# Attention's softmax transposed in float32 for two head pairs at a time, and cross attention queries over 512 weight columns

## The chip, the cores and the metric

The kernel runs on one core of a Trainium2 chip. The metric is the device time of one execution in microseconds (us), taken as the median of several runs. A profiled execution is traced beside them: every instruction on TensorE (PE; its weight loads are shown as PEld), VectorE (DVE), ScalarE (ACT), GpSimd (POOL) and on SyncE's DMA queue (SP), with its start, its duration and what ended the idle time before it. Line numbers such as L878 are those of the kernel before the change; the kernel after is a few lines shifted from `q_stream` on.

## The reference, cut to what matters

A two-layer decoder on 16 sequences of 64 tokens, width 512. Layer 0 has a causal attention with 32 query heads on 8 kv heads of width 128, a linear attention over channels with the context, and a gated ffn with group-scaled int4 weights. Layer 1 has an attention with ALiBi bias, a cross attention to the context and a base product with gated low-rank experts. A LayerNorm follows every block (post-LN). The part that the change touches is the attention of both layers and the queries of layer 1's cross attention:

```python
# attention, for every batch, kv head h and its four query heads g
s = einsum('bhgnd,bhmd->bhgnm', q, k) / sqrt(128) + mask    # 64 x 64
p = softmax(s, axis=-1)
o = einsum('bhgnm,bhmd->bhgnd', p, v)
x = layernorm(x + o @ wo.T)
# cross attention: the queries are normalised before the scores
q = rmsnorm(x @ q_proj_w.T)      # per head of 128
```

## The kernel before, in words

**Numbers.** Most products must be as good as float32, but TensorE works on fp32r, a rounded 32-bit type. A float32 matrix is therefore split into hi (rounded to fp32r, a cast on ACT) and lo (the exact rest, a subtraction on POOL or DVE). A product is then three matmuls, hi x hi + hi x lo + lo x hi (`mm3`, L101 to L107). `split_sb` (L84) splits from SBUF with ACT and POOL, `split_ps` (L89) from PSUM with ACT and DVE.

**Tiles.** The 1024 tokens are eight tiles of 128 (two batches each), in two halves of 512. SBUF tiles come from pools by tag, with a number of buffers each (`BUFS`, L34): `st` takes every loaded weight block before its split, `wq` and `wo` hold split weights, `s` and `p` softmax tiles, `pts` the transposed softmax, `ot` the attention's output split in hi and lo. PSUM has eight banks: two `mm`, three `fx`, one each of `sc` (scores), `pt` (transposes), `o` (product with V).

**Attention.** `Stream.run` (L970) walks a list of (layer, half of the tokens, kv head), two steps for each entry and four batches for a step: 32 steps for L0 and 64 for L1 (self attention, then cross attention), 96 in all. A step s does, in program order:
- projections of a later head (`units`), `fill` (work of other parts of the network that is spread over the steps),
- `pt(s, 0)`: four transposes of the softmax of two batches and a copy to `pts`; then the output projection `oproj(s - 1, 0)` of the step before (12 matmuls of 512 columns); then `av(s, 0)`, the product with V,
- more `fill` and projections, and the same for the other two batches: `pt(s, 1)`, `oproj(s - 1, 1)`, `av(s, 1)`,
- `scores(s + 2)`: 8 small matmuls and the softmax of the step after the next.

**Softmax.** `scores` (L847) leaves a tile `x` of [128 rows (two query heads, 64 queries), 8 (batch, pair of heads), 64 keys] in float32. The row maximum, the subtraction, exp, the sum and the division take DVE, ACT and POOL. Before the change, `x` is then split on ACT and POOL into `p`, hi and lo side by side on 128 columns (L871, L872). `pt` (L874) transposes each 128 x 128 block of `p` in fp32r, so that the hi of the 64 keys lands on partitions 0 to 63 and the lo on 64 to 127. V lies on both halves of the partitions, so one matmul over 128 partitions adds hi and lo.

**Cross attention queries.** `qn_front` (L790) computes the queries of one token tile for four heads in one bank, in two groups of 256 columns, one for each pair of heads: 24 matmuls of 256 columns. The weight `wqx` comes in two blocks a head, by pairs of query heads (L1056). ACT squares, DVE sums, POOL takes the power -1/2 and DVE multiplies (`rms`, L154); `qn_back` (L803) transposes.

**Linear attention.** `q_stream` (L359) runs chunks of 128 channels through five stages that lie 0, 1, 2, 4 and 5 ticks behind the first: logits, exp, norm, transpose, out (L430). Its tiles alternate between the tags `s` and `p` (L378). Beside the L0 ffn, a tile `acc` of tag `p` (L503) holds partial sums.

**Order.** Tile, the framework, puts the instructions of every engine into an order at build time, by priority and by when its own cost model expects operands to be ready. Softmax and the evacuations around it get a higher priority (`soon`, L74). Each engine then runs its list in that order. So the order on an engine is fixed before the run, and may differ from the program's.

## Time and profile before

Three runs took 2276.78, 2277.01 and 2281.83 us, median 2277.01. The profiled execution has a span of 2275.4 us from its first to its last instruction; the granted TensorE clock was 0.994 of full speed on average.

| stretch of the profiled execution (us) | what runs | PE busy | DVE | ACT | POOL |
|---|---|---|---|---|---|
| 0 to 45 | first loads and projections | 39.0 | 15.8 | 23.3 | 22.0 |
| 45 to 430 | L0 attention, keys of the linear attention | 382.5 | 221.1 | 231.5 | 159.4 |
| 430 to 740 | L0 attention, queries of the linear attention | 305.7 | 191.4 | 152.3 | 168.9 |
| 740 to 1150 | L0 ffn, rest of the queries, context keys and values | 381.6 | 337.1 | 214.4 | 230.2 |
| 1150 to 1660 | L1 self attention | 507.8 | 197.5 | 229.0 | 252.2 |
| 1660 to 2240 | L1 cross attention and L1 ffn | 564.2 | 357.8 | 267.6 | 336.0 |
| 2240 to 2276 | last LayerNorms and outputs | 27.8 | 25.4 | 6.0 | 4.2 |

Groups that matter below, with the number of instructions, the busy time in us and the mean duration of one in ns:

| line | engine, what | count | busy | mean |
|---|---|---|---|---|
| L878 | PE, fp32r transposes of p | 768 | 91.6 | 241 |
| L807 | PE, float32 transposes of queries | 256 | 38.5 | 273 |
| L105 | PE, hi x hi of the cross attention's queries, 256 columns | 512 | 149.3 | 292 |
| L889 | PE, product with V | 768 | 125.0 | 285 |
| L86 | ACT, hi of p | 96 | 59.6 | 620 |
| L87 | POOL, lo of p | 96 | 124.3 | 1295 |
| L881 | ACT, copy of the transposed softmax | 192 | 113.0 | 588 |
| L92 | DVE, lo of ot from PSUM | 192 | 132.0 | 687 |

How to read it: "busy" is the union of the durations in a group, and matmuls are pipelined, so the duration of one is longer than the distance to the next. Idle time is given before the instruction that ended it, with the releaser. On an engine that isn't the bottleneck idle time costs nothing.

### The profile page before, as it was taken

The page shows a single profiled execution, that of the slowest core. Times are in us where ns is not written, and L with a number is a line of the kernel's source. Part 1 is how long each engine was busy: PE and PEld are TensorE (multiplying, and loading weights), DVE is VectorE, ACT ScalarE, POOL GpSimd, SP SyncE. Part 2 cuts the span into 40 slices and gives each one's busy share as a digit, 9 for nine tenths or more (in the row PEclk, how much of TensorE's full clock was granted, in tenths as well). Part 3 has the DMA queues.
Part 4 walks back from the last instruction along what each step waited for, and adds up shares of the span by engine and source line. Part 5 has one row for each costly group of instructions (what it writes and reads, how often), then busy time and mean ns, then how long its engine had stood idle before and what let it go on. Part 6 is the DMA issues. An engine that isn't in the chain of part 4 may idle for free.

```text
span 2275.4 us, 36680 instructions
## 1 busy us (share of the span) xinstructions
PE 2208.5 (97%) x13200; PEld 1917.7 (84%) x13200; DVE 1346.0 (59%) x2523; ACT 1124.1 (49%) x2195; POOL 1172.9 (52%) x1001
## 2 busy tenths in 40 slices
PE   8999999999999999999999999999999999999998
PEld 7888888888888777777788888888898899988996
DVE  3655555667645789887743343433356566666656
ACT  5665556555444455555444444444444454443442
POOL 3533334455554655464654554545455666554641
PEclk9999999999999999999999999999999999999999
DMA  7533333322334322456543443334333343332320
GB/s 231 158 115 109 112 105 120 110 84 77 91 114 154 120 83 86 153 180 184 156 144 106 131 126 119 116 111 140 107 113 101 115 123 99 103 105 85 112 70 29
DMA packets 255317, 267.24 MB, mean 117 GB/s; under 512 B 32672, under 2 KB 168352, under 8 KB 255136
## 3 DMA queue, kind: packets, MB, share of 16 engines
q1 hardware_dynamic: 255136, 264.90, 38.1%
q8 instruction: 105, 1.72, 0.3%
q14 instruction: 76, 0.62, 0.1%
HBM read 231.26 MB, written 33.55 MB: 116 GB/s over the span
## 4 chain that ended last, share of the span: by engine, by line
PE 79%; DMA 5%; DVE 5%; POOL 5%; issue 2%; ACT 2%; SPq 0%; POOLq 0%; DVEq 0%; ACTq 0%
PE mm L105 16%; PE mm L106 15%; PE mm L107 15%; PE sc L856 6%; PE o L889 4%; PE fx L105 3%; PE fx L107 3%; PE fx L106 3%; PE pt L878 2%; DMA st<-in_down_s 1%; POOL wo L87 1%; PE fx L325 1%; POOL wq L87 1%; PE fx L298 1%; PE fx L316 1%
## 5 line engine op out<-in xcount | busy, mean ns | idle before, releaser
L87 POOL TENSOR_TENSOR wq<-st,wq 128x512 fp32r<-128x512 f32 x200 | 263.7, 1331 | 329.2 <-ACT wq L86 326.1
L107 PE MATMUL mm<-wo,ot 128*128 128x512 f32 x896 | 352.2, 393 | 0.0
L87 POOL TENSOR_TENSOR wo<-st,wo 128x512 fp32r<-128x512 f32 x226 | 296.6, 1342 | 96.8 <-ACT wo L86 88.0
L105 PE MATMUL mm<-wo,ot 128*128 128x512 f32 x768 | 315.2, 410 | 3.4 <-DVE x L904 3.1
L904 DVE TENSOR_TENSOR x<-x,mm 128x512 f32<-128x512 f32 x192 | 131.1, 683 | 308.2 <-PE mm L107 307.8
L106 PE MATMUL mm<-wo,ot 128*128 128x512 f32 x768 | 301.1, 392 | 0.0
L105 PE MATMUL mm<-xth,wq 128*128 128x512 f32 x512 | 204.9, 400 | 0.6 <-DVE v L92 0.3
L106 PE MATMUL mm<-xtl,wq 128*128 128x512 f32 x512 | 200.9, 392 | 0.0
L107 PE MATMUL mm<-xth,wq 128*128 128x512 f32 x512 | 200.6, 392 | 0.0
L107 PEld LDWEIGHTS mm<-wo,ot 128*128 128x128 f32 x896 | 169.3, 189 | 37.1
L91 ACT CAST ot<-o 128x512 fp32r<-128x512 f32 x192 | 112.3, 585 | 174.6 <-PE o L889 173.6
L114 POOL TENSOR_TENSOR r<-e,nhalf 128x4 f32<-128x4 f32 (+1 forms) x96 | 88.6, 923 | 203.2 <-DVE e L113 194.2
L86 ACT CAST wq<-st 128x512 fp32r<-128x512 f32 x204 | 123.8, 620 | 130.7 <-PE mm L106 73.5
L856 PEld LDWEIGHTS sc<-kt,qt 128*128 128x128 f32 x1536 | 184.4, 193 | 3.1
L856 PE MATMUL sc<-kt,qt 128*128 128x64 f32 x1536 | 185.0, 273 | 0.0
L92 DVE TENSOR_TENSOR ot<-o,ot 128x512 fp32r<-128x512 f32 x192 | 132.0, 687 | 81.8 <-ACT ot L91 81.5
L870 POOL TENSOR_TENSOR s<-s,rc 128x512 f32<-128x512 f32 x96 | 100.6, 1048 | 141.7 <-DVE rc L869 77.4
L105 PEld LDWEIGHTS mm<-wo,ot 128*128 128x128 f32 x768 | 144.6, 188 | 27.9 <-DVE x L904 3.4
L106 PEld LDWEIGHTS mm<-wo,ot 128*128 128x128 f32 x768 | 145.3, 189 | 24.1
L86 ACT CAST wo<-st 128x512 fp32r<-128x512 f32 x226 | 129.7, 624 | 41.0 <-PE mm L106 21.9
L105 PE MATMUL fx<-wq,xth 128*128 128x256 f32 x512 | 149.3, 292 | 0.0
L107 PE MATMUL fx<-wq,xtl 128*128 128x256 f32 x512 | 145.5, 284 | 0.0
(283 smaller groups left out, 5626.1 us busy)
## 6 DMA issues: line engine op xcount, KB each, us to landing
st<-in_wq SPq DMA_DIRECT2D x128, 256.0 KB, 3.1
st<-in_wo SPq DMA_DIRECT2D x128, 256.0 KB, 3.1
vs<-v SPq DMA_DIRECT2D x256, 128.0 KB, 3.1
v<-v SPq DMA_DIRECT2D x128, 128.0 KB, 2.7
st<-in_wqx SPq DMA_DIRECT2D x64, 256.0 KB, 2.9
st<-in_wox SPq DMA_DIRECT2D x64, 256.0 KB, 3.4
vs<-xv SPq DMA_DIRECT2D x128, 128.0 KB, 3.0
st<-in_gu_q SPq DMA_DIRECT2D x56, 256.0 KB, 3.0
```

What stands on the lines that cost most here:

```text
L86: self.nc.scalar.copy(hi, src)
L87: (self.nc.vector if fast else self.nc.gpsimd).tensor_tensor(lo, src, hi.bitcast(F32), ALU.subtract)
L91: self.nc.scalar.copy(hi, src)
L92: self.nc.vector.tensor_tensor(lo, src, hi.bitcast(F32), ALU.subtract)
L105: self.nc.tensor.matmul(out, lh, rh, start=first and i == 0, stop=False)
L106: self.nc.tensor.matmul(out, lh, rl, start=False, stop=False)
L107: self.nc.tensor.matmul(out, ll, rh, start=False, stop=last and i == n - 1)
L114: self.nc.gpsimd.tensor_tensor(out, e, self.nhalf[:, :n], ALU.pow)
L856: nc.tensor.matmul(sc[:, i * 64:(i + 1) * 64], qt[:, c + b, gp * 128:(gp + 1) * 128], kt[:, (c + b) * 64:(c + b + 1) * 64], start=True, st ...
L870: nc.gpsimd.tensor_tensor(x, x, rc.unsqueeze(2).to_broadcast([128, 8, 64]), ALU.mult)
L889: nc.tensor.matmul(o[:, b * 256:(b + 1) * 256], self.vs[s][i][:, bp * 2 + b], pts[:, b * 256:(b + 1) * 256], start=i == 0, stop=i == 1)
L904: self.nc.vector.tensor_tensor(n.x[t], n.x[t], ps, ALU.add)
```

## The change

The split of the softmax moves behind the transposition. `scores` leaves the normalised `x` in float32. `pt` is called once in a step: it transposes four blocks of 128 columns, each the two head pairs of one batch side by side, in float32. The transposed block then has the keys of one head pair on partitions 0 to 63 and those of the other on 64 to 127. For each pair, ACT copies its 64 partitions to fp32r as hi, and DVE writes the difference as lo to the other 64 partitions. So hi and lo again lie on the two halves, for the first pair in one order, for the second in the other. Both products with V of the step read from this tile.

The cross attention's query weights are arranged by halves of the input width instead of pairs of heads: a block has 2 of the 4 input parts and all 512 columns. `qn_front` is 12 matmuls of 512 columns.

Buffers: `st` 6 to 5, `s` 3 to 4, `ot` 4 to 3; a `pts` tile is twice as large. `q_stream` takes its softmax tiles from `p` alone, two chunks in one tile, and transposes three ticks behind the logits instead of four; `out` follows at four instead of five. The comments are gone from the file.

```diff
-BUFS = {"st": 6, "wq": 6, "wo": 6, "wk": 2, "wv": 2, "v": 4, "vs": 4, "qt": 2, "kt": 2, "s": 3, "p": 3, "pts": 2, "ot": 4}
+BUFS = {"st": 5, "wq": 6, "wo": 6, "wk": 2, "wv": 2, "v": 4, "vs": 4, "qt": 2, "kt": 2, "s": 4, "p": 3, "pts": 2, "ot": 3}
...
@@ q_stream, logits
-            s = live[c] = self.t(("s", "p")[c % 2], [128, 8, 64])
+            if c % 2 == 0:
+                cur["s"] = self.t("p", [128, 2, 8, 64])
+            s = live[c] = cur["s"][:, c % 2]
...
-        stages = ((5, out), (4, transpose), (2, norm), (1, exp), (0, logits))
+        stages = ((4, out), (3, transpose), (2, norm), (1, exp), (0, logits))
...
@@ qn_front
-        for gp in range(2):
-            w = self.wqs[h, gp]
-            n.mm3(ps[:, gp * 256:(gp + 1) * 256], [n.xt_slices(t, k) + (w[0][:, k], w[1][:, k]) for k in range(4)])
+
+        ws = [[flat(w).rearrange("p (k c) -> p k c", k=2) for w in self.wqs[h, kp]] for kp in range(2)]
+        n.mm3(ps, [n.xt_slices(t, k) + (ws[k // 2][0][:, k % 2], ws[k // 2][1][:, k % 2]) for k in range(4)])
...
@@ scores
-            x = n.t("s", [128, 8, 64])
+            x = self.p[s] = n.t("s", [128, 8, 64])
...
-            p = self.p[s] = n.t("p", [128, 8, 128], FR)
-            n.split_sb(x, p[:, :, 0:64], p[:, :, 64:128])
-
-    def pt(self, s, bp):
+
+    def pt(self, s):
+
         n, nc = self.n, self.nc
-        pt = n.bank("pt", FR)
-        for i in range(4):
-            nc.tensor.transpose(pt[:, i * 128:(i + 1) * 128], self.p[s][:, bp * 4 + i], n.identr)
-        pts = n.t("pts", [128, 512], FR)
+        pt, x = n.bank("pt"), self.p.pop(s)
+        for b in range(4):
+            nc.tensor.transpose(pt[:, b * 128:(b + 1) * 128], flat(x[:, 2 * b:2 * b + 2]), n.ident)
+        pts = n.t("pts", [128, 4, 256], FR)
         with n.soon():
-            nc.scalar.copy(pts, pt.bitcast(F32))
+            for gp in range(2):
+                r, q = slice(gp * 64, gp * 64 + 64), slice(64 - gp * 64, 128 - gp * 64)
+                src, c = pt[r].rearrange("p (b q) -> p b q", b=4), slice(gp * 128, gp * 128 + 128)
+                nc.scalar.copy(pts[r, :, c], src)
+                nc.vector.tensor_tensor(pts[q, :, c], src, pts[r, :, c].bitcast(F32), ALU.subtract)
         return pts
...
@@ av
-                                 pts[:, b * 256:(b + 1) * 256], start=i == 0, stop=i == 1)
+                                 pts[:, bp * 2 + b], start=i == 0, stop=i == 1)
...
@@ run
-            a = self.pt(s, 0)
+            a = self.pt(s)
...
-            a = self.pt(s, 1)
...
@@ _arrange
-    r["wqx"], r["wox"] = inout(i["L1_xattn_q_proj_w"].T, pairs), out(i["L1_xattn_o_proj_w"].T)
+    r["wox"] = out(i["L1_xattn_o_proj_w"].T)
...
+    r["wqx"] = inout(i["L1_xattn_q_proj_w"].T, KV).reshape(KV, 128, 2, 1024).transpose(0, 2, 1, 3)
```

More of the change, by code (lines that the diff above doesn't have):

```diff
@@ L1075, in _arrange @@
     r["b_base"], r["b_thr"] = i["L1_ffn_b_base"].reshape(1, D), i["L1_ffn_b_thr"].reshape(1, 1)
-    for n in ("wq0", "wq1", "wqx"):
+    for n in ("wq0", "wq1"):
         r[n] = r[n].reshape(KV, 2, 128, 1024)
+    r["wqx"] = inout(i["L1_xattn_q_proj_w"].T, KV).reshape(KV, 128, 2, 1024).transpose(0, 2, 1, 3)
     return {n: c(v) for n, v in r.items()}
```

## The prediction

> **What bounds the kernel now.** I read the engines' busy shares first, then the waits, then the timeline around the code that changes. The page's first part:

> ```profile
> span 2275.4 us, 36680 instructions
> PE 2208.5 (97%) x13200; PEld 1917.7 (84%) x13200; DVE 1346.0 (59%) x2523; ACT 1124.1 (49%) x2195; POOL 1172.9 (52%) x1001
> ```

> TensorE (PE) is busy 97% of the span, and the stage windows (0, 45, 430, 740, 1150, 1660, 2240 us) give it 382 of 385, 306 of 310, 382 of 410, 508 of 510 and 564 of 580 us. So a cut in PE's own work shortens the run directly, and a cut elsewhere only where PE waits. The idle 67 us lie mostly at the start, in the L0 ffn (740 to 1150 us, VectorE (DVE) 337 of 410 us busy) and in the cross attention (1660 to 2240). The page's durations of single matmuls overlap, so prices here are distances between starts. The timeline of PE shows both parts of the change in one look:

> ```profile
> 1703.26 0.28 PE L106 MATMUL fx<-wq,xth 128*128 128x256 f32 x1
> 1703.38 0.29 PE L107 MATMUL fx<-wq,xtl 128*128 128x256 f32 x1
> 1703.51 0.46 PE L878 MATMUL pt<-identr,p 128*128 128x128 f32 x4
> 1703.80 0.46 PE L105 MATMUL mm<-wo,ot 128*128 128x512 f32 x1
> 1704.10 0.39 PE L106 MATMUL mm<-wo,ot 128*128 128x512 f32 x1
> 1704.33 0.39 PE L107 MATMUL mm<-wo,ot 128*128 128x512 f32 x1
> ...
> 1713.08 0.64 PE L889 MATMUL o<-pts,vs 128*128 128x256 f32 x4
> 1713.55 0.60 PE L807 MATMUL fx<-ident,s 128*128 128x128 f32 x4
> 1713.91 0.36 PE L105 MATMUL fx<-wq,xth 128*128 128x256 f32 x1
> 1714.11 0.28 PE L106 MATMUL fx<-wq,xth 128*128 128x256 f32 x1
> ```

> A 256-column matmul follows the last after 0.12 us, a 512-column one after 0.23. Four fp32r transposes (L878) cost 1704.10 - 1703.38 - 0.12 - 0.23 = 0.37 us with the slow start of the matmul behind them; four float32 transposes (L807) cost 1714.11 - 1713.08 - 4 x 0.12 - 0.12 = 0.43 us. Between L878 and the product with V (L889) stand the 12 matmuls of an output projection: that product starts 2.65 us after the last transpose has ended, at most steps. ScalarE (ACT) and DVE around such a place, a cross attention step with L878 at 1690.64 and L889 at 1693.79:

> ```profile
> 1691.85 0.63 ACT L867 ACTIVATE s<-s 128x512 f32<-128x512 f32 x1 [1.42 <-DVE s L866]
> 1692.38 0.58 ACT L158 ACTIVATE s<-fx 128x512 f32<-128x512 f32 x1
> 1692.86 0.58 ACT L881 CAST pts<-pt 128x512 fp32r<-128x512 f32 x1
> ...
> 1690.03 1.79 DVE L866 TENSOR_TENSOR s<-s,mx 128x512 f32<-128x512 f32 x1
> 1692.51 0.69 DVE L868 TENSOR_REDUCE sm<-s 128x8 f32<-128x512 f32 x1 [0.70 <-ACT s L867]
> 1693.23 0.20 DVE L869 RECIPROCAL rc<-sm 128x8 f32<-128x8 f32 x1
> 1693.35 0.63 DVE L160 TENSOR_REDUCE ss<-s 128x4 f32<-128x512 f32 x1
> ```

> The copy of the transposed softmax (L881) stands on ACT behind an exp that itself waits for DVE; it ends at 1693.44, 0.35 us before PE wants it. That margin is what the change spends.

> **PE work, transposes.** 96 steps each give up two groups of fp32r transposes and get one of float32: 192 x 0.37 - 96 x 0.43 = 71 - 41 = **-30 us**; medians over all groups between 512-column matmuls (0.366 against 0.443, the latter from L136) give -28, which I take.

> **PE work, queries.** `qn_front` runs for 64 token tiles and heads: 24 x 0.12 = 2.88 us becomes 12 x 0.23 = 2.76, so 64 x 0.12 = **-8 us**. The weights' bytes, loads and casts stay. The second weight block is needed after 6 matmuls (1.4 us) rather than 12 x 0.12 = 1.4: no later and no earlier.
> [...]

> **Work taken off.** The hi cast of p on ACT (59.6 us in all) and its lo on GpSimd (124.3) go. PE's waits for that lo at L878 (4.5 us) go too, since x is ready sooner, and so do the waits of the second product of a step, which finds its operand long done (about 3.5 of the 8.4 us idle at L889): **-8 us**. L881 (192 x 0.59 us) is replaced by 192 ACT copies over 64 partitions; the nearest rows (L881, and L267 with 64 partitions at 616 ns) give the same 0.59. ACT and GpSimd have room, so the rest of their relief counts nothing.

> **Work put on.** 192 subtractions on DVE from PSUM. The nearest row is L92 (ot, PSUM and SBUF, 687 ns); L268, 64 partitions but both inputs in SBUF, gives 1061 and is the upper end. At 0.69 DVE gains 132 us, 59% to 65% of the span, hidden under PE outside the L0 ffn, where there is no attention.

> **The new wait.** av(s, 0) now needs four evacuations. From the start of the first copy: copy 0.59, the second starts at about 0.53 (ACT spacing, as L867 to L158), the first subtraction runs from 0.62, the second from 1.23 (DVE spacing 0.6), the end is at 1.92, and 0.05 until PE sees it: 1.97 us. The first copy starts after the last transpose's end, in the timeline, by 0.73 us at most L0 steps beside the keys' stream, by 0.23, 0.54 or 1.08 in L1's self attention, by about 1.77 at even and 0.93 at odd cross attention steps. Against 2.65 us of cover that makes: even cross steps 1.1 x 16 = 17, odd ones 0.25 x 16 = 4, self attention 0.4 x 8 = 3, L0 4: **+28 us**. Behind the waiting product stand on PE all projections, so each us counts.
> Low end 0: the order on PE is planned, and at some steps (near 496, 527, 553, 629 us) 18 to 28 matmuls lie between L878 and L889 instead of 12, so a wait that the planner foresees is filled. High end 100: if the four evacuations go one after another (2 x 0.59 + 2 x 0.69 + hand-overs = 2.7) and L160 stands ahead of the subtraction, 0.6 to 1.4 us more per step over 96 steps. I take 28, near the low end, because the steps above show the planner at work and only ACT's lateness at the cross steps is beyond it.
> No row has ACT and DVE on one PSUM bank at once. [...]

> **Buffers and order.** st goes from 6 to 5. The chain of waits runs through st loads of 3 to 5 us each between 713 and 1130 us (in_gu_s, in_down_s), and those come four at a time for one unit of down weights. Bounds: 0, since PE idles only 28 us there, to 15, about half as much again; I take **+4**. ot with 3: av(s, 1) reuses what oproj(s-1, 0) has freed half a step before, no wait. s with 4: two softmaxes and two query tiles at most, freed by PE just ahead of need, nothing; DVE's 53 us of waits for s (L861 behind POOL) should go, off the path. q_stream's transposition comes one tick earlier (ticks are 2 to 8 us, about 4.6); the normalised tile is mostly ready 3 to 10 us ahead now, so a few of the 64 chunks come late: 0 to 8 us, taken as **+2**. DMA issues on SP keep their number and order.

> **Sum.** -28 - 8 - 8 + 28 + 4 + 2 = -10 us on a profiled span of 2275.4 us. The median of the three runs, 2277.0, is 1.6 us above that span; I predict against the median: **2267 us** (-0.4%). Own range of this case 2255 to 2274.

> **Rivals.**
> Full gain: the planner fills the waits, or GpSimd's lighter load shortens L866 (1.79 us here, 1.00 on average), so exp and copies come earlier. Stall 3 rather than 28: 2242 us (2230 to 2255). For it: the 18 to 28 matmuls above; against it: at 17 of the 32 cross steps L881 ends less than 0.4 us before L889 already.
> The evacuation decides (slower): ACT to DVE to PE in front of av(s, 0). The gains are 44, other costs 6, so it turns at 38/96 = 0.40 us of stall per step; at 0.75 us (serial evacuation, partly filled) 72 us: 2311 us (2284 to 2330). For it: L889 already waits for L881 up to 2.45 us at 1777.4; against it: L1's self attention has 0.7 to 1.8 us to spare.
> The gain is real but st and q_stream's shorter lag take it back in the L0 ffn, +14 instead of +6, with a stall of 30: 2277 us (2270 to 2284). For it: the chain through st; against it: loads are issued well ahead outside the down weights.

> **How the numbers follow.** Chances: forecast 0.42, full gain 0.22, evacuation 0.26, buffers 0.10. A change within 0.3% (7 us) can't be told from none. Two thirds of the forecast's own range lie below 2270, and all of the full gain's: faster 0.28 + 0.22 = 0.50. Same is the rest of the forecast and six tenths of the buffers, 0.14 + 0.06 = 0.20; slower 0.26 + 0.04 = 0.30. The 8-in-10 range leaves out half of the full gain (0.11) and a third of the evacuation (0.09): 2240 to 2314.

> **What would show it.** Right: PE busy near 2170 us, L807-like spacing (0.36 us) in the pt group, 0.23 us between query matmuls; idle before L889 of 20 to 35 us in all, released by DVE pts, mainly at even cross steps. Wrong: idle at L889 over 60 us, or none; PE's idle in 740 to 1150 us well above 28; pt groups dearer than 0.5 us.

## The result, and the profile after

The changed kernel takes 2337.3 us (median of four runs, 2323.59 to 2338.99) against 2276.9 us for the kernel before (four runs on the same chip): a ratio of 1.0249, 95% interval 1.022 to 1.0278. It is slower by 60 us. The prediction was 2267 us, faster by 0.4%, with a range of 2240 to 2314.

The first part of the page of the kernel after, with its span and the engines' busy shares:

```profile
span 2334.9 us, 34278 instructions
...
PE 2200.4 (94%) x12048; PEld 1857.1 (80%) x12048; DVE 1468.8 (63%) x2715; ACT 1091.6 (47%) x2099; POOL 1048.7 (45%) x905
```

PE has 1152 matmuls fewer than before and is busy only 8 us less, while the span has grown by 59.5. So PE idles 68 us more: 127.7 us, found by adding up its gaps between instructions, against 60.2 before. To see where, the execution can be cut at the additions to the residual (DVE L909, L904 before), which both kernels make in the same order:

| stretch | length before | after | PE idle before | after | idle just before the product with V, before | after |
|---|---|---|---|---|---|---|
| L0 attention (to the 64th addition) | 759.7 | 761.0 | 12.8 | 21.2 | 1.0 | 7.6 |
| L0 ffn (to the 65th) | 435.1 | 460.9 | 30.6 | 47.7 | 0 | 0 |
| L1 self attention (to the 129th) | 549.7 | 554.5 | 1.3 | 12.6 | 1.2 | 12.5 |
| L1 cross attention and ffn (to the 188th) | 484.0 | 512.6 | 12.5 | 44.2 | 6.2 | 41.9 |
| end | 47.0 | 45.9 | 3.0 | 2.1 | 0 | 0 |

Two places stand out: the cross attention, whose idle lies almost wholly in front of the product with V, and the L0 ffn, where attention runs only in the last 30 us. The groups of instructions of the kernel after (busy us, mean ns of one, then the idle time just before them and what ended it):

```profile
L894 PE MATMUL o<-pts,vs 128*128 128x256 f32 x768 | 132.8, 295 | 62.0 <-DVE pts L886 39.4 <-issue 21.5 <-DVE ot L92 0.5
...
L879 PE MATMUL pt<-ident,s 128*128 128x128 f32 x384 | 58.0, 272 | 0.0
```

The transposes (L879) are half as many and wait for nothing any more. The product with V (L894) idles PE 62.0 us, where the product before (L889) had 8.4. For 39.4 us of it the releaser is the lo subtraction that the change put on DVE. For another 21.5 the profile names none ("issue"), but there too the product starts within 0.3 us of the end of the last subtraction. Of the 96 steps 46 wait in this way. The list of waits of the kernel after (engine, tile and line that wait, what released them, total us, times, longest) shows the path behind it:

```profile
DVE pts L886 <- ACT pts L885: 71.4, 89, 2.8
ACT pts L885 <- DVE pts L886: 70.9, 73, 1.9
...
DVE s L162 <- POOL r L114: 54.5, 61, 1.2
PEld o L894 <- DVE pts L886: 53.9, 49, 3.3
...
PE o L894 <- DVE pts L886: 39.4, 23, 2.9
```

ACT's copy waits for DVE's subtraction nearly as long as the subtraction waits for the copy. The two engines alternate on one bank. One cross attention step of the kernel after, by the timeline of ACT, DVE, POOL and PE, in this order:

```profile
1931.51 0.63 ACT L869 ACTIVATE s<-s 128x512 f32<-128x512 f32 x1 [1.43 <-DVE s L868]
1932.05 0.58 ACT L158 ACTIVATE s<-fx 128x512 f32<-128x512 f32 x1
1932.52 0.57 ACT L885 CAST pts<-pt 64x512 fp32r<-64x512 f32 x1
1934.40 0.58 ACT L885 CAST pts<-pt 64x512 fp32r<-64x512 f32 x1 [1.31 <-DVE pts L886]
...
1933.01 0.64 DVE L160 TENSOR_REDUCE ss<-s 128x4 f32<-128x512 f32 x1
1933.68 0.69 DVE L886 TENSOR_TENSOR pts<-pt,pts 64x512 fp32r<-64x512 f32 x1
1934.40 0.17 DVE L113 TENSOR_SCALAR e<-ss 128x4 f32<-128x4 f32 x1
1935.69 0.69 DVE L162 TENSOR_TENSOR s<-fx,r 128x512 f32<-128x512 f32 x1 [1.12 <-POOL r L114]
1936.41 0.69 DVE L886 TENSOR_TENSOR pts<-pt,pts 64x512 fp32r<-64x512 f32 x1
...
1934.65 1.01 POOL L114 TENSOR_TENSOR r<-e,nhalf 128x4 f32<-128x4 f32 x1 [0.36 <-DVE e L113]
...
1933.57 0.60 PE L809 MATMUL fx<-ident,s 128*128 128x128 f32 x4
...
1934.46 0.40 PE L107 MATMUL mm<-wo,ot 128*128 128x512 f32 x1
1937.16 0.75 PE L894 MATMUL o<-pts,vs 128*128 128x256 f32 x4 [2.30 <-DVE pts L886]
```

The reader can follow the late operand backwards. The second subtraction ends at 1937.10 and PE starts at 1937.16, after 2.30 us of nothing. That subtraction could have run from 1934.98, when the second copy ended. It stands on DVE behind the scaling of a query tile (L162), which waits 1.12 us for POOL's power (L114) and then takes 0.69. The second copy in turn waited 1.31 us for the first subtraction, and that one stood behind the query tile's sum (L160). The four transposes themselves had long been done.

This step is no exception. In all 96 steps the second copy starts only after the first subtraction has ended. From the start of the first copy to the end of the last subtraction it takes 3.5 us on average: 3.1 in L0, 3.0 in the self attention and 4.3 in the cross attention, where the prediction had 1.92.

### The profile page after: what moved, and what is told of

It reads as the page before. It is cut to its first block, busy times and chain, and to the rows that moved or that the text cites. A ratio compares the mean times of both kernels' runs of the same rounds, so it can differ in the third digit from the quotient of the medians.

```text
span 2334.9 us, 34278 instructions
## 1 busy us (share of the span) xinstructions
PE 2200.4 (94%) x12048; PEld 1857.1 (80%) x12048; DVE 1468.8 (63%) x2715; ACT 1091.6 (47%) x2099; POOL 1048.7 (45%) x905
## 5 line engine op out<-in xcount | busy, mean ns | idle before, releaser
L87 POOL TENSOR_TENSOR wq<-st,wq 128x512 fp32r<-128x512 f32 x200 | 268.5, 1353 | 349.8 <-ACT wq L86 346.3
L107 PE MATMUL mm<-wo,ot 128*128 128x512 f32 x896 | 352.9, 394 | 0.0
L87 POOL TENSOR_TENSOR wo<-st,wo 128x512 fp32r<-128x512 f32 x226 | 291.1, 1317 | 129.8 <-ACT wo L86 128.5
L105 PE MATMUL mm<-wo,ot 128*128 128x512 f32 x768 | 312.2, 406 | 0.8 <-ACT qt L790 0.8
L106 PE MATMUL mm<-wo,ot 128*128 128x512 f32 x768 | 302.4, 394 | 0.0
L909 DVE TENSOR_TENSOR x<-x,mm 128x512 f32<-128x512 f32 x192 | 131.7, 686 | 195.0 <-PE mm L107 191.6
L105 PE MATMUL mm<-xth,wq 128*128 128x512 f32 x512 | 205.2, 401 | 0.7 <-ACT kt L779 0.6
L107 PE MATMUL mm<-xth,wq 128*128 128x512 f32 x512 | 201.4, 393 | 0.0
L106 PE MATMUL mm<-xtl,wq 128*128 128x512 f32 x512 | 201.3, 393 | 0.0
L114 POOL TENSOR_TENSOR r<-e,nhalf 128x4 f32<-128x4 f32 (+1 forms) x96 | 88.3, 920 | 249.6 <-DVE e L113 238.1
L107 PEld LDWEIGHTS mm<-wo,ot 128*128 128x128 f32 x896 | 170.2, 190 | 37.2
L894 PE MATMUL o<-pts,vs 128*128 128x256 f32 x768 | 132.8, 295 | 62.0 <-DVE pts L886 39.4
L894 PEld LDWEIGHTS o<-pts,vs 128*128 128x128 f32 x768 | 112.6, 191 | 97.1 <-DVE pts L886 53.9
L92 DVE TENSOR_TENSOR ot<-o,ot 128x512 fp32r<-128x512 f32 x192 | 132.4, 690 | 91.1 <-ACT ot L91 89.2
L86 ACT CAST wq<-st 128x512 fp32r<-128x512 f32 x204 | 124.3, 621 | 138.7 <-PE mm L106 64.3
L886 DVE TENSOR_TENSOR pts<-pt,pts 64x512 fp32r<-64x512 f32 x192 | 132.2, 689 | 74.7 <-ACT pts L885 71.4
L105 PEld LDWEIGHTS mm<-wo,ot 128*128 128x128 f32 x768 | 146.2, 190 | 28.2 <-ACT qt L790 1.0
L106 PEld LDWEIGHTS mm<-wo,ot 128*128 128x128 f32 x768 | 146.3, 191 | 26.9
```

The lines of the kernel that those rows point to most:

```text
L86: self.nc.scalar.copy(hi, src)
L87: (self.nc.vector if fast else self.nc.gpsimd).tensor_tensor(lo, src, hi.bitcast(F32), ALU.subtract)
L92: self.nc.vector.tensor_tensor(lo, src, hi.bitcast(F32), ALU.subtract)
L105: self.nc.tensor.matmul(out, lh, rh, start=first and i == 0, stop=False)
L106: self.nc.tensor.matmul(out, lh, rl, start=False, stop=False)
L107: self.nc.tensor.matmul(out, ll, rh, start=False, stop=last and i == n - 1)
```

## The experiments

All times are medians, each against the kernel before on the same chip, whose median there lay between 2276.6 and 2280.3 us. Line numbers are those of the kernel in question.

**The queries alone.** The kernel before with `qn_front` over 512 columns, and the weights arranged to fit:

```diff
-        for gp in range(2):
-            w = self.wqs[h, gp]
-            n.mm3(ps[:, gp * 256:(gp + 1) * 256], [n.xt_slices(t, k) + (w[0][:, k], w[1][:, k]) for k in range(4)])
+        ws = [[flat(w).rearrange("p (k c) -> p k c", k=2) for w in self.wqs[h, kp]] for kp in range(2)]
+        n.mm3(ps, [n.xt_slices(t, k) + (ws[k // 2][0][:, k % 2], ws[k // 2][1][:, k % 2]) for k in range(4)])
```

> The kernel before with the queries' part alone (12 matmuls of 512 columns, weights by halves of the input width). Theory A (the loss comes from the wait in front of av(s, 0) and from the L0 ffn's stretch): 2269 us, 8 less than before, since 64 x 0.12 us of TensorE work go and nothing else is late. Rival (the queries' wider matmuls themselves bring waits, for the second weight block or the bank): 2277 or more.

Measured: 2266.7 us against 2280.25, ratio 0.9947 (0.9932 to 0.9962). Faster by 13.6 us. In the profile the stretch of the cross attention is 9.2 us shorter, 1.7 of which is one slow spell of PE's clock less (see the last section); the L0 attention, which the edit does not touch, is 3 us shorter, again with fewer slow spells. The term of -8 stands.

**One `st` buffer less, alone.** The kernel before with this one edit:

```diff
-BUFS = {"st": 6, ...
+BUFS = {"st": 5, ...
```

> The kernel before with five st buffers, nothing else. Theory A: 2275 to 2281 us. Rival B (starved loads cost the L0 ffn's stretch): 2295 to 2303 us.

Measured: 2309.0 us against 2280.25, ratio 1.0127 (1.011 to 1.0144), 29 us slower, more than either theory had. The waits of this kernel, the three largest for an `st` load and those of the product with V:

```profile
ACT wq L86 <- DMA st<-in_wqx: 36.6, 22, 3.2
ACT wq L470 <- DMA st<-in_gu_q: 32.9, 22, 4.4
PEld o L889 <- ACT pts L881: 26.6, 29, 2.4
ACT wq L86 <- DMA st<-in_wq: 26.1, 26, 3.9
...
PE o L889 <- ACT pts L881: 15.4, 12, 2.0
```

In the kernel before the same five rows are 11.1, 21.4, 12.6, 24.9 and 6.1 us. Over all loads, ACT waits 145.5 us for `st` (120 times) instead of 94.9 (87 times). ACT runs its list in order, so a weight cast whose block has not landed holds up the copy of the transposed softmax behind it, and PE waits at L889: 9.4 of the 24.5 us that PE idles more lie there. The loss lies in every stretch: L0 attention +8.4, L0 ffn +15.6, self attention +3.2, cross attention +6.7. The prediction had looked only at the L0 ffn.

**`q_stream`'s part alone, and the change without it.** The first kernel is the one before with the two edits of `q_stream` (tiles from `p`, shorter lags), the second the changed kernel with both undone, the third the changed kernel with the lags alone undone:

```diff
-            s = live[c] = self.t(("s", "p")[c % 2], [128, 8, 64])
+            if c % 2 == 0:
+                cur["s"] = self.t("p", [128, 2, 8, 64])
+            s = live[c] = cur["s"][:, c % 2]
...
-        stages = ((5, out), (4, transpose), (2, norm), (1, exp), (0, logits))
+        stages = ((4, out), (3, transpose), (2, norm), (1, exp), (0, logits))
```

> The kernel before with q_stream's change alone (tiles two by two from p, stages 4 and 3). If taking all of q_stream's tiles from the three p buffers starves the L0 ffn's partial sums (first partial sums wait 9 to 13 us for a buffer where both run): 2287 to 2297 us, the loss in the stretch of the L0 ffn alone. Here attention's own p tiles come on top beside L0's second half, so it may be more. If that loss needs the five st buffers beside it: 2275 to 2281 us.

> The changed kernel with q_stream as before (tiles from s and p in turn, stages 5 and 4). Theory A (q_stream's shorter lag and its tiles all from p cost the 26 us that the stretch between L0 attention's end and L1's first output projection lost): about 2311 us, and that stretch back near 435 us. Rival B (the five st buffers cost them): about 2337 us, the stretch stays near 461 us.

> The changed kernel with q_stream's stages back at 5 and 4, its tiles still all from p. If the shorter lag cost the 16 us that the old q_stream gave back: about 2321 us, waits of L400 for GpSimd's norm (7.4 us) gone. If the sharing of the p buffers with the L0 ffn's partial sums cost them: 2337 us or more, with waits of L507 for L510 (8.6 us) kept or grown.

Measured: the part alone 2300.4 us against 2276.6, ratio 1.0088 (1.0062 to 1.0114), +24 us, of which the L0 ffn stretch has 18 and the L0 attention 7. The change without it 2321.6 against 2280.25, ratio 1.0191 (1.0174 to 1.0208), that is 19 us less loss than the full change; its L0 ffn stretch is 448.3 us, only half of the way back to 435. A part of these differences is PE's clock (see the last section): PE spends 52.5 us at half speed in the first kernel (28.4 before), and 41.1 in the second (59.0 with the full change), which can make up to 12 of the 24 and 9 of the 19 us. The change with the old lags 2336.0 against 2277.6, ratio 1.0267 (1.0239 to 1.0296), so nothing is won back by the lags.

So it is the tiles. All chunks now come from tag `p`, which has three buffers and also holds the partial sums of the L0 ffn. In the kernel after, the first partial sum of four successive ffn tiles (ACT, L510) starts 17.0, 9.1, 12.6 and 8.6 us after its matmuls, between 835 and 905 us; before, 19.3, 3.5, 1.2 and 4.1. The delays go with the tiles: 16.6, 9.1, 13.9 and 9.2 us in the kernel before with `q_stream`'s part, 19.1, 3.5, 1.2 and 4.1 in the changed kernel without it. PE then finds the bank of the partial product still full. Two waits of the kernel after, the second of which is for `q_stream`'s transposition:

```profile
PE o L507 <- ACT p L510: 8.6, 6, 1.9
...
PE fx L400 <- POOL p L394: 7.6, 7, 2.7
```

Before, the first was 1.6 us (L505 behind L508). With the old lags the second is gone from PE's list (it waits 4.9 us there for the chunk's subtraction instead), and the first is still 7.8 us.

**The order of the four evacuations.** The changed kernel with both copies issued before both subtractions, so that a subtraction no longer stands between the copies and the two subtractions are neighbours:

```diff
                 nc.scalar.copy(pts[r, :, c], src)
+            for gp in range(2):
+                r, q = slice(gp * 64, gp * 64 + 64), slice(64 - gp * 64, 128 - gp * 64)
+                src, c = pt[r].rearrange("p (b q) -> p b q", b=4), slice(gp * 128, gp * 128 + 128)
                 nc.vector.tensor_tensor(pts[q, :, c], src, pts[r, :, c].bitcast(F32), ALU.subtract)
```

> The changed kernel with both ACT copies of a step issued ahead of both DVE subtractions; same instructions. Theory A (the second subtraction stands on DVE behind L162, which waits for GpSimd, and the copies alternate with the subtractions on one bank): idle in front of the product with V falls from 62 us to about 30, 2295 to 2310 us. Rival (it is only the first copy that comes late, behind the exp): idle stays over 50 us, over 2325 us.

Measured: 2332.9 us against 2277.6, ratio 1.0246 (1.022 to 1.0272). Nothing is won, and a gain of some 30 us was expected; time and idle are as the rival had them. Yet the alternation is gone, as the timeline of the same step shows (ACT, DVE, PE):

```profile
1943.55 1.16 ACT L885 CAST pts<-pt 64x512 fp32r<-64x512 f32 x2
...
1944.75 1.39 DVE L889 TENSOR_TENSOR pts<-pt,pts 64x512 fp32r<-64x512 f32 x2
...
1944.59 0.38 PE L809 MATMUL fx<-ident,s 128*128 128x128 f32 x2
1946.24 0.72 PE L897 MATMUL o<-pts,vs 128*128 128x256 f32 x4 [1.27 <-issue]
```

From the first copy to the product it now takes 2.69 us, not 4.64, and over all steps the evacuations take 2.8 us on average instead of 3.5. But PE's list has changed as well: behind the 12 matmuls of the output projection stand only two query transposes in front of the product, no longer four and three matmuls more. Counted over all steps, the median number of PE instructions in between is 13.5 here, 16 in the changed kernel (12 before the change). The order is planned with modelled times. The likely reason, which no run isolates, is that with shorter evacuations the plan puts the product earlier, and that what the model does not foresee is left over either way: at the cross steps the first copy starts 1.2 us after the last transpose here, 0.7 us in the changed kernel. 57.2 us of idle stay at the product instead of 62.0.

**The transposition earlier.** The changed kernel with `pt(s)` ahead of the step's own projections and fill instead of behind them:

```diff
+            a = self.pt(s)
             for u in units[0]:
                 u()
             fill(s, 0)
-            a = self.pt(s)
```

> The changed kernel with pt(s) called ahead of the step's first projections, so that more TensorE work lies between the transposes and av(s, 0). Theory A (the four evacuations, one after another and with the second subtraction behind a waiting instruction, stand in front of av): idle in front of L894 falls from 62 us to under 15, the half-speed windows of the cross attention go, about 2270 us; the L0 ffn's stretch stays 26 us too long. Rival C (the planned order as such is worse everywhere, by chance): over 2315 us, the idle only moves to other lines.

Measured: 2267.2 us against 2280.25, ratio 0.9945 (0.993 to 0.9961). From 60 us slower to 13 us faster, by moving one line. The group of the product with V in this kernel:

```profile
L894 PE MATMUL o<-pts,vs 128*128 128x256 f32 x768 | 125.0, 285 | 6.2 <-issue 3.3 <-DVE ot L92 1.1 <-PE mm L107 1.0
```

The number of PE instructions in between is now 24 or more at most steps. The evacuations are as slow as before, 3.4 us on average, but the product starts 2.4 us after their end. So the cover was too short, whatever made the chain long. The self and cross attention stretches are 537.8 and 464.2 us, 12 and 20 us below the kernel before. The L0 ffn is untouched by it: 459.2.

**The three losses taken back together.** First the early transposition with the old `q_stream`, then with six `st` buffers as well. In the second, room in SBUF comes from dropping the fp32r identity (unused after the change), a single-use tile and 8 of 44 small tiles, and from loading the cross attention's mask into the tile of L0's causal mask. A third kernel is the second with `pt(s)` back where the change has it.

```diff
-BUFS = {"st": 5, ...
+BUFS = {"st": 6, ...
...
-        self.identr = self.const.tile([128, 128], FR, name="identr")
-        nc.vector.tensor_copy(self.identr, self.ident)
...
-            kx = st[i][0] = ex.tile([128, 256], F32, name="lkx", bufs=1)
+            kx = st[i][0] = self.t("v", [128, 256])
...
-            ax.mask = self.const.tile([128, 64], F32, name="xmask")
+            ax.mask = a0.mask
```

> The changed kernel with pt(s) ahead of the step's first projections and with q_stream as before, st still 5. If the two losses add up (the wait in front of av 70 us, q_stream 14 to 16 us, as measured one at a time): 2251 to 2255 us. If q_stream's part only shifted which wait ends last: near 2267 us.

> The same with six st buffers, the room for them taken from the unused fp32r identity, the second mask tile, lkx (now in the v buffers) and eight of the 44 small tiles. If the sixth st buffer is worth in this kernel what it is worth in the kernel before (about 30 us): 2220 to 2228 us. If its worth there was due to the old attention's loads and casts: 2245 to 2255 us.

> The changed attention and queries, q_stream as before, six st (room made as in the version with early transposition), pt(s) where the change has it. Against that version (2234) only the place of pt differs. Theory A (the wait in front of av costs 60 to 70 us): 2292 to 2300 us, idle in front of the product with V near 60 us. If the five st, whose late loads hold ScalarE up, made most of the wait: 2250 to 2270 us.

Measured: 2258.9 us against 2277.6, ratio 0.9924 (0.9906 to 0.9942); with six buffers **2233.9 us** (2231.18 to 2237.79), ratio 0.981 (0.9794 to 0.9826), which beats both kernels; with the transposition late again 2315.5 against 2276.6, ratio 1.016 (1.0135 to 1.0185). The first two are 4 and 6 us slower than a plain sum of the losses would have it; the third is 15 us slower than the upper end expected. The page and the product's group of the 2233.9 us kernel:

```profile
span 2236.0 us, 34238 instructions
...
PE 2172.0 (97%) x12048; PEld 1854.1 (83%) x12048; DVE 1467.1 (66%) x2714; ACT 1089.6 (49%) x2099; POOL 1039.1 (46%) x905
```

```profile
L890 PE MATMUL o<-pts,vs 128*128 128x256 f32 x768 | 124.6, 284 | 5.7 <-issue 2.4 <-DVE ot L90 1.6 <-DVE pts L882 1.5
```

and the same group with the transposition late:

```profile
L890 PE MATMUL o<-pts,vs 128*128 128x256 f32 x768 | 133.7, 297 | 63.5 <-DVE pts L882 39.1 <-issue 22.2 <-DVE ot L90 0.8
```

PE busy 2172 us is 36.5 less than before the change: the predicted saving of the transposes and queries (28 + 8) is there in full. The place of one line decides 82 us (83 when each run is compared with the kernel before on its own chip).

**Is it only the earlier transposition?** The kernel before with the queries over 512 columns and `pt(s, 0)` moved up in the same way; the softmax is still split before the transposition:

```diff
+            a = self.pt(s, 0)
             for u in units[0]:
                 u()
             fill(s, 0)
-            a = self.pt(s, 0)
```

> The kernel before with the queries' part and with pt(s, 0) ahead of the step's first projections; softmax split as before, six st. It shows what the earlier transposition is worth without the change's other half. If TensorE's saving from four float32 instead of eight fp32r transposes is real (28 us): no faster than 2258 us, some 20 to 28 us behind the version with the moved split, early transposition and six st (2234). If that version owed its time to the earlier transposition alone: near 2240 us.

Measured: 2274.2 us against 2276.6, ratio 0.9984 (0.9971 to 0.9997). That is 40 us above the best kernel, and some 11 us worse, relative to the kernel before, than the queries alone; up to 8 of these 11 us can be PE's clock (39.9 us at half speed instead of 22.9). The earlier place is worth nothing to the old split. The moved split, with its wait covered, is worth about 40 us (2274.2 - 2233.9; this pair also differs in the numbers of `s` and `ot` buffers and in the edits that made room).

## Why the prediction was wrong, point by point

The chain of one-step differences, each kernel by its distance to the kernel before on its own chip, gives the size of each term in two orders:

| from the kernel before (0) to | distance, us | step |
|---|---|---|
| moved split and queries, `pt` early, old `q_stream`, `st` 6 | -43.8 | -43.8 |
| then `st` 5 | -18.7 | +25 |
| then `q_stream` new | -13.1 | +6 |
| then `pt` where the change has it | +60.4 | +73 |
| other order: `pt` late first | +39.0 | +83 |
| then `st` 5 | +41.4 | +2 |
| then `q_stream` new (the change) | +60.4 | +19 |

By the intervals of the ratios each step is known to some 5 to 8 us, so +2 can't be told from nothing, and +6 only just. The steps "then `st` 5" also take back the small edits that made room for six.

- **Work taken off PE and waits removed, -28 - 8 - 8 = -44: right.** -43.8 measured once the other losses are out of the way. That it agrees so closely is partly luck: PE is busy 36.5 us less, but the waits at the transposes fall from 4.5 to 1.8 us and those at the product from 8.4 to 5.7, 5.4 rather than 8, and the profiled execution is 39.4 us shorter. In the kernel after the saving does not show: PE is busy 2200.4 us, not near 2170. Half-speed spells of its clock, 59.0 us instead of 28.4, can hide up to 15 of the 28 us that are missing; the rest is not accounted for. In the kernel after, queries follow each other after 0.23 us, and a group of four transposes takes 0.35 us to the next instruction; both are as predicted.
- **The new wait, +28: the step that failed.** The mechanism was named (four evacuations before `av(s, 0)`, worst at the cross steps), and the sign was turned by its size: idle at the product is 62.0 us rather than 20 to 35, and the step costs 73 to 83. The prediction had 21 us for the cross steps, 3 for the self attention and 4 for L0; the trace shows 41.9, 12.5 and 7.6. Three things were missing. It took the second copy to start 0.53 us after the first, beside the subtraction; it started 1.7 us after on average (1.88 in the step shown above), behind it, at every step. The prediction had named four evacuations one after another as its high end, and reckoned with the other order, which no row of the kernel before showed. It took the subtractions to run when their operands were there; the second stood behind L162, which waits for POOL. And it took the planner to fill most of the rest, because it had seen 18 to 28 matmuls at some steps. The planner did put 16 instead of 12 instructions in between (median), but the lateness of ACT and DVE was left over; that the planner fills only what its model foresees is what the reordered evacuations suggest. Which of the three weighs most is not shown, since the earlier transposition covers them all. The high end of 100 in the prediction described the chain that was measured. In the step shown above the second copy (the other 64 partitions) waited 1.31 us for the first subtraction. The two instructions share the bank `pt` and the tile `pts`, on separate parts of both. In one place of the kernel after, separate parts of an SBUF tile did not wait for each other: ACT writes one part of `xth` (L86) from 41.97 us while DVE reads another (L87), 0.61 us side by side. That the two engines take turns because of the bank is the author's estimate from these two places; no run isolates it.
- **`st` 6 to 5, +4: wrong in size**, 25 to 29 us with the early `pt` and in the kernel before. The failed step is "PE idles only 28 us there": it bounded the cost by the L0 ffn, while the loads of all layers pass through `st` and delay ACT, on which the softmax evacuations stand. With the late `pt` in place it costs only 2 us more; why so little I did not find.
- **`q_stream`, +2: wrong**, 6 to 24 us. The prediction priced the shorter lag, which costs nothing measurable, and not the move of half of the tiles from `s` to `p`, where the L0 ffn's partial sums live.
- **Buffers `s` 4 and `ot` 3: nothing speaks against it**, PE waits 0.5 us in all for `ot` at the product; no run has them alone. DVE's waits behind POOL for `s` (53 us) did not go: 46.4 us remain, off the path.
- **The subtraction's price, 0.69 us on DVE: right**, 0.689.

Both signs that were named as proof against the forecast are in the profile after: idle of 62.0 us at the product, and 43.6 us idle in 740 to 1150 us, where it was 28.4 before. The rival "the evacuation decides" was the right one, with 2311 us (up to 2330) for 0.26. It was short of 2337 because it left `st` and `q_stream` at +6. The losses measured each alone do not add up: 83 + 29 + 24 makes 136, while the kernel loses 104 (and gains 44). Each edit lets the whole order be planned anew, and two waits may cover each other.

## What to carry to other kernels

When a change puts an evacuation chain over two engines between two matmul groups, don't price the chain by its own durations: look in the timeline at what stands ahead of each link on its engine and what that in turn waits for, and check whether the cover is fixed by a planner that knows only modelled times. If the chain is long, issue its head earlier in program order; here one line moved was worth 73 to 83 us. And a staging buffer taken away to make room is priced over every stretch in which an in-order engine waits for its loads, and a tile tag by all its users.

## What the runs showed of the hardware that was not expected

```profile
1933.30:1936.70 3.40, 1.55 (x9) 0.96 (x7) 2.19 (x5) 1.78 (x3) 2.73 (x3) 1.00 0.23 77
1936.70:1940.10 3.40, 2.94 (x16) 2.59 (x17) 1.90 (x4) 1.92 (x4) 1.45 (x2) 1.00 0.24 77
1967.40:1970.80 3.40, 1.38 (x9) 0.82 (x7) 2.19 (x5) 1.78 (x3) 2.78 (x3) 1.00 0.22 77
1970.80:1974.20 3.40, 3.12 (x9) 2.68 (x10) 1.60 (x3) 1.59 (x3) 0.61 (x2) 0.50 0.24 77
```

The first gap is cut by a slot's border and leaves 1.79 us in one slot: the clock stays at 1.00. The second leaves 2.0 us in one slot and the clock in the next is 0.50. An estimate from these figures: 3.41 us at 0.50 lose up to 1.7 us, so the kernel before loses up to 14 us in this way and the kernel after up to 29, and the difference is a quarter of its 60 us. The stall of 2.30 us at 1968.78 can so have cost up to 4.0 us.
